# A four-layer graph network on one core: the first two groups of graphs interleaved, the last group finished by pairs

## The chip, the cores and the metric

The kernel runs on one core of a Trainium2 chip. The metric is the device time in microseconds (us), given as the median of the runs. The engines are named as in the profile: PE is TensorE's matmul, PEld its weight load, DVE is VectorE, ACT is ScalarE, POOL is GpSimd and SP is SyncE, which here issues nearly all DMAs. All data is fp32.

## The reference

`x` holds 128 graphs of 128 nodes with 512 features, `adj` their 128x128 adjacency matrices. Four layers follow one another, each as `x = layernorm(x + layer(x, adj))`, cut here to what is computed:

```python
# layer 0
Ah = A + I;  dh = rsqrt(sum(Ah, -1));  An = dh[:, :, None] * Ah * dh[:, None, :]
out = relu(einsum('bnm,bmf,fc->bnc', An, X, kernel) + bias)
# layer 1
q, k = split(x @ W_qk.T);  v = x @ W_v.T;  scores = q @ k.T / 8
out = softmax(sum(scores * A, -1), axis=nodes) * v
# layer 2
agg = (A @ x) / max(sum(A, -1), 1e-6)
out = relu(concat([x, agg]) @ W.T)
# layer 3
out = An @ (X @ W + b)
```

## The kernel before, in words

**Groups.** The 128 graphs are worked on in 32 groups of `G` = 4; the features of a group's four graphs lie in one SBUF tile `x` of 128 nodes by 4 x 512. A group goes through all four layers on chip, and is then stored.

**A layer.** `aggregate` (L441) multiplies x by the transposed adjacency matrix, so that the result comes out with the features on the partitions, as the next product needs it, and ScalarE copies it from PSUM (`agg<-p_agg`). Where a layer needs x itself in that form (layers 1 and 2), x has to be transposed: `turn_x` (L450) stores it to a scratch tensor in DRAM (`xT1s`, `xT2s`), loads it back in another order (`xT1y`, `xT2y`), and VectorE transposes blocks of 32x32. The adjacency matrices are transposed by TensorE for groups 0 and 1 (`prep_transpose`, L412, PSUM tile `p_a`) and by the same way over DRAM for the others (`prep_turn`, L423). `prep_rows` (L389) makes the scaled matrices: VectorE sums the degrees (`deg`, `dh`), GpSimd raises them to the power -1/2 (`d`), and VectorE multiplies (`ana`).

**A projection.** `project` (L482) is one step of a seven-product scheme (Strassen-Winograd): the two halves of the rows (graphs 0, 2 against 1, 3: the index `r`; `q` counts the pairs of graphs 0, 1 and 2, 3) and of the features make blocks, and seven products named B11, T1, B21, B22, T2, T3, T4 take the place of eight. Their left operands are sums made by `left_sums` (L464; GpSimd as a rule, tiles `xT1s`, `agg2s` and so on), their right ones sums of weight blocks made once by `weight_sums` (L359). Each product adds into a PSUM region `p_o` or `p_v`; VectorE combines the regions (`u_o`, `s_o`), adds to x, and takes the statistics of the layer norm (`norm_stats`, L568: VectorE `bno`, GpSimd `rstdo` and `mro`, ScalarE `nmro` and the scaling of x). For layer 3 ScalarE takes the statistics itself (`norm_last`, L550: `row`, `square`). The last product, T4, is put off: `project` leaves it in a list of tails, and the next projection runs it after its own first product (`finish_tails`). In PE's rows, `w_sb` stands for w0 and w3, so `p_o<-w_sb,agg` belongs to layer 0 or 3 by its time.

**The order of the work.** Every instruction is first recorded, then `Plan.schedule` (L192) puts them in order. TensorE's order is the program's. The other engines, the DMA issues on SP among them, take at each step the instruction that is ready and due first; a due time is counted back from TensorE's order with the costs of `estimate` (L279). A DMA counts 470 ns on SP and 1600 ns + size / 60 until it has landed, whatever else is under way. All planned instructions show line L258 in the profile.

The main loop (L764) runs over t and mixes group t with group u = t - 1: layer 0 of t, layer 2 of u (with the first half of t's qk), the aggregation of t + 1, layer 1 of t, the aggregation and projection of layer 3 of u, then x of t transposed over DRAM and aggregated for layer 2. So each group's norms and transposes have another group's products beside them. The ends have no such neighbour: before the loop group 0 is prepared and aggregated alone, at t = 0 only layers 0 and 1 of group 0 run, with group 1's preparation, and at t = 32 only layers 2 and 3 of group 31.

The loads: `load` (L334) brings `adj` and `x` of a group on SP's queue, `weight` (L344) a weight as four blocks of 256 KB or, turned, as 16 of 64 KB. w0 and b0 are issued by ScalarE, all else by SP.

Of the kernel before, what the change touches and what calls it, by code (L numbers as in the profile page):

```python
# [24 lines left out]
DEG_EPS = 1e-6  # L25

# [92 lines left out]
class Op:  # L119
    def __init__(self, engine):  # L120
        self.engine, self.dur, self.lat, self.calls, self.preds, self.succs = engine, 0, 0, [], set(), []
        self.last, self.start, self.end = float("inf"), None, None


class Plan:
# [5 lines left out]
    HOP = 200  # L131

# [22 lines left out]
    def record(self, engine, method, args, kw):  # L155
        op = self.group if self.group is not None and engine == "tensor" else Op(engine)
        op.calls.append((method, args, kw))
        dur, op.lat = self.est(engine, method, args, kw)
# [33 lines left out]
    def schedule(self):  # L192
# [24 lines left out]
        free = dict.fromkeys(self.ENGINES, 0)  # L217
# [5 lines left out]
        while len(done) < len(self.ops):  # L223
# [18 lines left out]
            free[e] = op.end  # L242
            if e == "tensor":
                pe.pop(0)
# [34 lines left out]
def estimate(engine, method, args, kw):  # L279
# [3 lines left out]
    if engine == "tensor":  # L283
        return (max(109, 0.85 * n) if method == "transpose" else 2 * max(100, 0.833 * n + 2.5)), 100
    if method == "dma_start":
        size = max(int(np.prod(v.shape)) if isinstance(v, bass.AP) else v.idx.size * 32 * len(v.quads) for v in args)
        return 470, 1600 + size / 60
    if engine == "scalar":
        return (380 if method == "activation" else 160) + 0.83 * n, 0
    if engine == "gpsimd":  # L290
        if ALU.pow in args:
            return 400 + 150 * n, 0
        return 250 + 2.2 * n, 0
# [3 lines left out]
    return 160 + (1.3 if len(both) > 1 else 1.04) * n, 0  # L297
# [4 lines left out]
def kernel(  # L302
# [15 lines left out]
    NT = B // G  # L318

# [14 lines left out]
    def load(t):  # L334
# [3 lines left out]
        nc.sync.dma_start(xi, x[t * G:(t + 1) * G].rearrange("g n f -> n g f"))  # L338
# [32 lines left out]
    make_identity(tc.nc, ident.real())  # L371
    nhalf = const.tile([P, G], FP, tag="nhalf", name="nhalf")
    nc.vector.memset(nhalf, -0.5)
    w0_sb = weight(w0, "w0_sb", nc.scalar)
    b0_sb = broadcast_row(b0, "b0_sb", nc.scalar)
# [88 lines left out]
    def left_sums(name, t, eng=nc.gpsimd):  # L464

        a = st[name, t].rearrange("p (q r) (h c) n -> p q r h c n", r=2, h=2)
        a11, a12, a21, a22 = a[:, :, 0, 0], a[:, :, 0, 1], a[:, :, 1, 0], a[:, :, 1, 1]
        s1, s2, s3, s4 = (tp.tile([P, 2, 2, P], FP, tag=f"s{i}", name=f"{name}s{i}_{t}", bufs=3) for i in (1, 2, 3, 4))
        eng.tensor_tensor(s1, a21, a22, ALU.add)
        eng.tensor_tensor(s2, s1, a11, ALU.subtract)  # L470
        eng.tensor_tensor(s3, a11, a21, ALU.subtract)
        eng.tensor_tensor(s4, a12, s2, ALU.subtract)
        st[name, t] = {B11: a11, B21: a12, B22: s4, T4: a22, T1: s1, T2: s2, T3: s3}
# [8 lines left out]
    def project(name, t, parts, first, c11, fin, hooks=None, after=lambda: None, early=True,  # L482
                when=lambda f: f()):
# [3 lines left out]
        hooks = hooks or {}  # L487

        def region():
            return ps_b.tile([P, 2, H], FP, tag="pb", name=f"p_{name}_{t}")  # L490

        def product(p, k, fresh):
            with nc.unit():
                for q in range(2):
                    for i, (left_, w) in enumerate(parts):
                        for c in range(2):
                            nc.tensor.matmul(p[:, q, :], left_[k][:, q, c, :], w[:, k, c, :],
                                             start=(fresh and q == 0 and i == 0 and c == 0),
# [4 lines left out]
        def block(tag):  # L503
            return tp.tile([P, 2, H], FP, tag=tag, name=f"{tag}_{name}_{t}", bufs=1 if tag in ("u5", "sb") else 2)
# [21 lines left out]
        when(lambda: (fin(0, 1, u2), norm_stats(name, t, 0)))  # L526
# [4 lines left out]
        def tail():  # L531
# [3 lines left out]
            norm_stats(name, t, 1)  # L535
# [4 lines left out]
    def half(z, r, h):  # L540

        return z.rearrange("p (q r) f -> p q r f", r=2)[:, :, r, h * H:(h + 1) * H]
# [7 lines left out]
    def norm_last(name, t, r):  # L550

        z = st["x", t]
        sm, nm, sq, rstd, nmr = (sp.tile([P, 2], FP, tag=f"last{i}", name=f"last{i}_{t}_{r}", bufs=2) for i in range(5))
        for q in range(2):
            row = tp.tile([P, F], FP, tag="row", name=f"row_{t}_{r}_{q}", bufs=1)
            nc.scalar.activation(row, z[:, 2 * q + r, :], AF.Copy, accum_out=sm[:, q:q + 1])
        nc.scalar.mul(nm, sm, -1.0 / F)
        for q in range(2):
            row = tp.tile([P, F], FP, tag="row", name=f"square_{t}_{r}_{q}", bufs=1)
            nc.scalar.activation(row, z[:, 2 * q + r, :], AF.Square, bias=nm[:, q:q + 1], accum_out=sq[:, q:q + 1])  # L560
        nc.gpsimd.tensor_scalar(rstd, sq, 1.0 / F, LN_EPS, ALU.mult, ALU.add)
        nc.gpsimd.tensor_tensor(rstd, rstd, nhalf[:, 0:2], ALU.pow)
        nc.gpsimd.tensor_tensor(nmr, nm, rstd, ALU.mult)
        for q in range(2):
            zg = z[:, 2 * q + r, :]
            nc.scalar.activation(zg, zg, AF.Identity, bias=nmr[:, q:q + 1], scale=rstd[:, q:q + 1])

    def norm_stats(name, t, r):  # L568
        if name == "o3":
            return norm_last(name, t, r)  # L570
        z = st["x", t]
        mv = sp.tile([P, 2, 2], FP, tag="mv", name=f"mv{name}_{t}_{r}")
        for q in range(2):
# [6 lines left out]
        nc.gpsimd.tensor_scalar(rstd, mv[:, :, 1], LN_EPS, None, ALU.add)  # L580
        nc.gpsimd.tensor_tensor(rstd, rstd, nhalf[:, 0:2], ALU.pow)
        nc.gpsimd.tensor_tensor(mr, mv[:, :, 0], rstd, ALU.mult)
        nc.scalar.mul(nmr, mr, -1.0)
        for q in range(2):
            zg = z[:, 2 * q + r, :]
            nc.scalar.activation(zg, zg, AF.Identity, bias=nmr[:, q:q + 1], scale=rstd[:, q:q + 1])


    def l0_agg(t, eng=nc.gpsimd):
# [3 lines left out]
        left_sums("agg0", t, eng)  # L593

    def relu_add(t):
        def fin(r, h, blk):
            z = half(st["x", t], r, h)
# [3 lines left out]
    def bias(h):  # L601
        return b0_sb[:, None, h * H:(h + 1) * H].to_broadcast([P, 2, H])

    def l0_out(t, hooks=None):
# [236 lines left out]
```

## Time and profile before

| What | Value |
|---|---|
| median of 3 runs | 2537.95 us (2536.98 to 2547.46) |
| profiled execution, own time | 2536.82 us |
| its span, first to last instruction | 2535.0 us |
| mean granted TensorE clock | 0.991 |
| DMA, mean over the span | 98 GB/s, 249.62 MB |
| PE busy in the first 60 us | 32.1 us |
| PE busy in the last 75 us (2460 to 2535) | 51.6 us |

The profile is one execution. A span row gives the busy time of each engine; a row of stretches gives the same for a part of the span, with the clock that TensorE was granted as a share of full speed. A wait row says which engine stood idle before which work, and what released it. A row of the timeline has the start, the length, the engine, the operation, out<-in with its shapes, the count, and in brackets the idle time just before. TensorE's rows count two instructions for each fp32 matmul of the program, and one for each transpose.

The first PE instruction starts at 12.42 us, the first product of layer 0 at 19.06. From 90.23 us PE works without a gap up to the steady part. At the end, the aggregation for layer 2 of the last group starts at 2460.58, the last matmul ends at 2521.47, ScalarE's last scaling at 2529.33, and the store of the last group's 1 MB lands at the span's end.

### The profile page before, as it was taken

To read this page: it belongs to the slowest core of one execution; us is meant where nothing else is said; L and a number is where in the kernel's file an instruction comes from. 1 tells how busy PE (TensorE), PEld (TensorE's weight loads), DVE (VectorE), ACT (ScalarE), POOL (GpSimd) and SP (SyncE) were. 2 spreads that over 40 slices of the span, in tenths; PEclk is the share of its full clock that TensorE was granted. 3 is DMA by queue.
4 is the path that set the end of the run, shared out by engine and by line. 5 is a ranking of instruction groups with operands and counts; after the bars stand their busy time and mean duration, and the time that the engine had idled before them with its cause. 6 is when DMAs were issued, how large, how long until landed. Compare 5 with 4: busy or idle time off the path is not lost.

```text
span 2535.0 us, 36875 instructions
## 1 busy us (share of the span) xinstructions
PE 2464.3 (97%) x13392; PEld 2201.8 (87%) x13392; DVE 1777.4 (70%) x3141; ACT 962.0 (38%) x1955; POOL 1354.6 (53%) x1522
## 2 busy tenths in 40 slices
PE   5899999999999999999999999999999999999996
PEld 4788888888888888888888888888988888888885
DVE  5677767776767776777777777767677767677663
ACT  1243334343334433343433343433443433344333
POOL 6455456464555564555554564655564645555542
PEclk8999999999999999999999999999999999999998
DMA  7233334324344324343333344233343243433120
GB/s 220 75 81 95 101 100 121 109 63 112 88 112 111 102 72 117 83 121 108 87 89 109 92 121 108 72 104 99 102 121 107 65 113 84 116 109 95 39 84 33
DMA packets 408532, 249.62 MB, mean 98 GB/s; under 512 B 141344, under 2 KB 375328, under 8 KB 408352
## 3 DMA queue, kind: packets, MB, share of 16 engines
q1 hardware_dynamic: 407120, 245.96, 36.0%
q8 instruction: 106, 1.74, 0.3%
q10 hardware_dynamic: 1232, 1.31, 0.2%
q14 instruction: 74, 0.61, 0.1%
HBM read 130.81 MB, written 116.39 MB: 98 GB/s over the span
## 4 chain that ended last, share of the span: by engine, by line
PE 75%; DVE 9%; DMA 5%; POOL 4%; issue 3%; SPq 2%; ACT 1%; ACTq 0%; DVEq 0%; POOLq 0%
PE p_o L258 45%; PE p_v L258 13%; PE p_agg L258 12%; DVE x L258 4%; PE p_qk L258 3%; SPq L258 2%; POOL xT2s L258 2%; ACT x L258 1%; DMA xT1y<-xT1s 1%; DMA adj<-in_adj_dram 1%; DVE u_o L258 1%; DMA xT1s<-x 1%; DVE s_v L258 1%; DVE ana L258 1%; DVE bnv L258 1%
## 5 line engine op out<-in xcount | busy, mean ns | idle before, releaser
L258 ACT COPY agg<-p_agg 128x512 f32<-128x512 f32 x384 | 224.9, 586 | 722.1 <-PE p_agg L258 722.1
L258 PE MATMUL p_o<-w_sb,agg 128*128 128x256 f32 x1536 | 354.8, 380 | 4.2 <-DVE u_o L258 2.2
L258 PEld LDWEIGHTS p_o<-w_sb,agg 128*128 128x128 f32 x1536 | 287.4, 191 | 42.6 <-ACT s_o L258 3.2
L258 POOL TENSOR_TENSOR xT1s<-xT 128x512 f32<-128x512 f32 x64 | 83.1, 1298 | 394.5 <-DVE xT L258 306.7
L258 POOL TENSOR_TENSOR agg3s<-agg 128x512 f32<-128x512 f32 x64 | 86.5, 1351 | 338.9 <-ACT agg L258 338.9
L258 PE MATMUL p_o<-w2x_sb,xT2s 128*128 128x256 f32 x1024 | 262.8, 379 | 0.0
L258 PE MATMUL p_o<-w2a_sb,agg2s 128*128 128x256 f32 x1024 | 262.8, 379 | 0.0
L258 PE MATMUL p_agg<-anT,x 128*128 128x128 f32 x2048 | 249.4, 281 | 10.0 <-ACT x L258 4.5
L258 PEld LDWEIGHTS p_agg<-anT,x 128*128 128x128 f32 x2048 | 240.2, 195 | 11.6 <-DVE anT L258 5.1
L258 PE MATMUL p_o<-w_sb,agg3s 128*128 128x256 f32 x1024 | 233.4, 381 | 5.6 <-DVE u_o L258 5.5
L258 PE MATMUL p_v<-wv_sb,xT1s 128*128 128x256 f32 x1024 | 233.3, 381 | 0.0
L258 PE MATMUL p_o<-w_sb,agg0s 128*128 128x256 f32 x1024 | 226.6, 379 | 2.9 <-DVE agg0s L258 1.9
L258 PEld LDWEIGHTS p_o<-w_sb,agg3s 128*128 128x128 f32 x1024 | 192.1, 190 | 41.7 <-POOL rstdv L258 16.8
L258 PEld LDWEIGHTS p_o<-w_sb,agg0s 128*128 128x128 f32 x1024 | 194.3, 190 | 30.1 <-POOL sb_o L258 2.2
L258 PEld LDWEIGHTS p_o<-w2x_sb,xT2s 128*128 128x128 f32 x1024 | 194.6, 190 | 26.5
L258 PEld LDWEIGHTS p_o<-w2a_sb,agg2s 128*128 128x128 f32 x1024 | 194.6, 190 | 26.4
L258 PEld LDWEIGHTS p_v<-wv_sb,xT1s 128*128 128x128 f32 x1024 | 189.6, 190 | 25.9
L258 POOL TENSOR_TENSOR agg2s<-agg 128x512 f32<-128x512 f32 x64 | 81.2, 1268 | 233.3 <-ACT agg L258 233.3
L258 PE MATMUL p_o<-w2x_sb,xT 128*128 128x256 f32 x768 | 198.3, 381 | 3.8 <-DVE xT L258 3.1
L258 DVE STREAM_TRANSPOSE xT<-xT1y 128x512 f32<-128x512 f32 x128 | 83.5, 690 | 168.4 <-DMA xT1y<-xT1s 168.4
L258 PE MATMUL p_o<-w2a_sb,agg 128*128 128x256 f32 x768 | 197.8, 380 | 0.0
L258 ACT ACTIVATE x<-x,nmro,rstdo 128x512 f32<-128x512 f32 x256 | 194.6, 807 | 4.8 <-ACT nmro L258 0.5
(116 smaller groups left out, 4705.8 us busy)
## 6 DMA issues: line engine op xcount, KB each, us to landing
x<-in_x_dram SPq DMA_DIRECT2D x32, 1024.0 KB, 6.2
xT1s<-x SPq DMA_DIRECT2D x128, 256.0 KB, 2.7
xT1y<-xT1s SPq DMA_DIRECT2D x256, 128.0 KB, 3.0
xT2s<-x SPq DMA_DIRECT2D x128, 256.0 KB, 2.6
xT2y<-xT2s SPq DMA_DIRECT2D x256, 128.0 KB, 3.3
out_dram<-x SPq DMA_DIRECT2D x32, 1024.0 KB, 5.5
sa<-ana SPq DMA_DIRECT2D x120, 128.0 KB, 3.4
ya<-sa SPq DMA_DIRECT2D x120, 128.0 KB, 3.7
```

Source lines behind the costliest of these rows:

```text
L258: getattr(getattr(self.nc, op.engine), method)(*[v.real() if isinstance(v, Ref) else v for v in args], **{k: v.real() if isinstance(v, Ref ...
```

## The change

- **First groups** (`begin`). Group 0 is prepared and its layer 0 starts; group 1's transposes and its aggregation lie between group 0's products of layer 0 (after B21 and B22). Then comes group 1's layer 0, ahead of group 0's layer 1. x of group 0 is transposed on TensorE for layers 1 and 2 (`turn_on_tensor`: a ScalarE copy that reorders the columns, four TensorE transposes into PSUM, a ScalarE copy out of it, for each graph), and `l2_both` mixes these transposes with the aggregation. qk of group 1 comes before that. The loop then starts at t = 1 without layer 0 and qk of group 1; its order from t = 2 on is the same.
- **Last group.** x of group 31 is transposed on TensorE (`l2_both`, with the sums of xT2 on VectorE). Layer 2 and layer 3 are run by pairs of graphs: 0, 1 first and then 2, 3, each with its own seven products of half the size. Each graph is stored as soon as it is scaled. The very last norm takes its statistics on VectorE.
- **Loads.** w0 and b0 are issued by SP too, x of group 0 comes in two halves, and the planner counts the DMAs on SP as sharing one bus of 95 elements per ns.
- **Clock.** 30 transposes of the identity matrix are put ahead of the first work of TensorE.
- Layer 0's sums for group 0 are made pair by pair.

```diff
+WARM = 30
...
+    LAND, BUS = 1600, 95
...
+            if e == "sync":
+                bus = max(bus, op.end + self.LAND) + op.size / self.BUS
+                op.lat = max(op.lat, bus - op.end)
...
-        return 470, 1600 + size / 60
...
         if ALU.pow in args:
...
-        nc.sync.dma_start(xi, x[t * G:(t + 1) * G].rearrange("g n f -> n g f"))
+        for g in range(0, G, 2 if t == 0 else G):
+            k = slice(g, g + (2 if t == 0 else G))
+            nc.sync.dma_start(xi[:, k], x[t * G:(t + 1) * G][k].rearrange("g n f -> n g f"))
...
+    p = ps_t.tile([P, C, P], FP, tag="pt", name="p_warm")
+    for _ in range(WARM):
+        nc.tensor.transpose(p[:, 0], ident, ident)
...
-    w0_sb = weight(w0, "w0_sb", nc.scalar)
-    b0_sb = broadcast_row(b0, "b0_sb", nc.scalar)
+    w0_sb = weight(w0, "w0_sb", nc.sync)
+    b0_sb = broadcast_row(b0, "b0_sb", nc.sync)
...
+    def turn_on_tensor(name, t, r, pairs=(0, 1)):
+
+        y = tp.tile([P, 2, C, P], FP, tag="y", name=f"{name}y_{t}_{r}", bufs=3)
+        for q in pairs:
+            g = 2 * q + r
+            z = y[:, q]
+            nc.scalar.copy(z.rearrange("p c (b j) -> p c b j", b=Q),
+                           st["x", t][:, g, :].rearrange("p (b c j) -> p c b j", b=Q, c=C))
+            p = ps_t.tile([P, C, P], FP, tag="pt", name=f"p_{name}_{t}_{g}")
+            with nc.unit():
+                for c in range(C):
+                    nc.tensor.transpose(p[:, c, :], z[:, c], ident)
+            nc.scalar.copy(st[name, t][:, g], p)
+
+    def left_sums(name, t, eng=nc.gpsimd, pairs=(slice(0, 2),)):
...
+        s = [tp.tile([P, 2, 2, P], FP, tag=f"s{i}", name=f"{name}s{i}_{t}", bufs=3) for i in (1, 2, 3, 4)]
+        for q in pairs:
+            a11, a12, a21, a22 = a[:, q, 0, 0], a[:, q, 0, 1], a[:, q, 1, 0], a[:, q, 1, 1]
+            s1, s2, s3, s4 = (v[:, q] for v in s)
+            eng.tensor_tensor(s1, a21, a22, ALU.add)
+            eng.tensor_tensor(s2, s1, a11, ALU.subtract)
+            eng.tensor_tensor(s3, a11, a21, ALU.subtract)
+            eng.tensor_tensor(s4, a12, s2, ALU.subtract)
+        st[name, t] = {B11: a[:, :, 0, 0], B21: a[:, :, 0, 1], B22: s[3], T4: a[:, :, 1, 1], T1: s[0], T2: s[1], T3: s[2]}
...
-                for q in range(2):
+                for q in pairs:
                     for i, (left_, w) in enumerate(parts):
                         for c in range(2):
-                            nc.tensor.matmul(p[:, q, :], left_[k][:, q, c, :], w[:, k, c, :],
-                                             start=(fresh and q == 0 and i == 0 and c == 0),
+                            nc.tensor.matmul(p[:, q - pairs[0], :], left_[k][:, q, c, :], w[:, k, c, :],
+                                             start=(fresh and q == pairs[0] and i == 0 and c == 0),
                                              stop=(i == len(parts) - 1 and c == 1), skip_group_check=True)
...
-        when(lambda: (fin(0, 1, u2), norm_stats(name, t, 0)))
+        when(lambda: (fin(0, 1, u2), norm_stats(name, t, 0, pairs)))
...
-            norm_stats(name, t, 1)
+            norm_stats(name, t, 1, pairs)
             after()
...
+        for q in pairs:
             zg = z[:, 2 * q + r, :]
             nc.scalar.activation(zg, zg, AF.Identity, bias=nmr[:, q:q + 1], scale=rstd[:, q:q + 1])
-
-    def norm_stats(name, t, r):
-        if name == "o3":
-            return norm_last(name, t, r)
+            if t == last:
+                nc.sync.dma_start(out[t * G + 2 * q + r], zg)
+
+    def norm_stats(name, t, r, pairs):
+        if name == "o3" and (t, r, pairs[-1]) != (last, 1, 1):
...
+        for q in pairs:
             zg = z[:, 2 * q + r, :]
             nc.scalar.activation(zg, zg, AF.Identity, bias=nmr[:, q:q + 1], scale=rstd[:, q:q + 1])
-
-
-    def l0_agg(t, eng=nc.gpsimd):
+            if name == "o3":
+                nc.sync.dma_start(out[t * G + 2 * q + r], zg)
...
         left("xT1", t)
         for r in range(2):
-            turn_x("xT1", t, r)
+            turn("xT1", t, r)
...
+
+        left("xT2", t)
+        left("agg2", t)
+        for r in range(2):
+            turn_on_tensor("xT2", t, r)
+            for g in (r, 2 + r):
+                aggregate("agg2", t, g, st["arT", t])
+        left_sums("xT2", t, nc.vector)
+        left_sums("agg2", t)
...
+    def l3_agg_pair(t, q, eng):
+        left(f"agg3{q}", t)
+        for g in (2 * q, 2 * q + 1):
+            aggregate(f"agg3{q}", t, g, st["anT", t])
+        left_sums(f"agg3{q}", t, eng, ONE_BY_ONE[q:q + 1])
...
+        project("o3", t, [(st[left, t], w3_sb)], copy_first, lambda p, b: fin(0, 0, p), fin,
+                after=lambda: store(t), pairs=pairs)
 
     def store(t):
+        if t == last:
+            return
         nc.sync.dma_start(out[t * G:(t + 1) * G].rearrange("g n f -> n g f"), st["x", t])
...
-    prep_rows(0)
-    load(1)
-    prep_transpose(0)
-    weight_sums(w0_sb, nc.gpsimd)
-    l0_agg(0, nc.vector)
...
-    for t in range(NT + 1):
...
+    def begin():
+
+        prep_rows(0)
+        load(1)
+        prep_transpose(0)
+        weight_sums(w0_sb, nc.gpsimd)
+        l0_agg(0, nc.vector, ONE_BY_ONE)
+        prep_rows(1)
+        l0_out(0, {B21: [lambda: prep_transpose(1)], B22: [lambda: l0_agg(1)]})
+        finish_tails()
+        weight_sums(wv_sb, nc.vector)
+        l0_out(1)
+        l1_turn(0, turn_on_tensor)
+        finish_tails()
+        for r in range(2):
+            l1_qk(0, r)
+        for w in (w2x_sb, w2a_sb, w3_sb):
+            weight_sums(w, nc.gpsimd)
+        l1_turn(1)
+        l1_out(0, {B11: [lambda: l1_scores(0)], B21: [lambda: l1_softmax(0)], T3: []})
+        finish_tails()
+        for r in range(2):
+            l1_qk(1, r)
+        l2_both(0)
+
+    begin()
+    for t in range(1, NT):
...
-        if a:
+        if t > 1:
             l0_out(t)
-        if more:
-            if b:
-                load(t + 1)
+        if t < last:
+            load(t + 1)
             prep_rows(t + 1)
-            if b:
-                prep_turn(t + 1)
-        if a:
+            prep_turn(t + 1)
+        if t > 1:
             tails.append(lambda: l1_turn(t))
-        if a and b:
-            l2_out(u, {T3: [lambda: l1_qk(t, 0)]})
-        elif b:
-            l2_out(u)
-        else:
-            weight_sums(wv_sb, nc.vector)
-            for w in (w2x_sb, w2a_sb, w3_sb):
-                weight_sums(w, nc.gpsimd)
-            finish_tails()
-            prep_transpose(t + 1)
-        if more:
+        l2_out(u, {T3: [lambda: l1_qk(t, 0)]} if t > 1 else {})
+        if t < last:
             l0_agg(t + 1)
         finish_tails()
-        if a:
-            if not b:
-                l1_qk(t, 0)
+        if t > 1:
             l1_qk(t, 1)
-        if a:
-            l1_out(t, {B11: [lambda: l1_scores(t)], B21: [lambda: l1_softmax(t)],
-                       T3: [lambda: l3_agg(u)] if b else []})
-        elif b:
-            l3_agg(u)
-        if b:
-            l3_bias(u)
-            l3_out(u)
-        else:
-            finish_tails()
-        if a:
+        l1_out(t, {B11: [lambda: l1_scores(t)], B21: [lambda: l1_softmax(t)], T3: [lambda: l3_agg(u)]})
+        l3_bias(u)
+        l3_out(u)
+        if t < last:
             l2_turn(t)
             l2_agg(t)
+
+    l2_both(last)
+    for q in range(2):
+        l2_out(last, pairs=(q,))
+    for q in range(2):
+        l3_agg_pair(last, q, nc.gpsimd)
+        l3_bias(last, (2 * q, 2 * q + 1))
+        l3_out(last, f"agg3{q}", (q,))
     finish_tails()
```

## The prediction

> **What bounds the kernel now.** I read the busy shares first, then the busy time by stretches, then the waits of TensorE, then its timeline at both ends.
>
> ```profile
> PE 2464.3 (97%) x13392; PEld 2201.8 (87%) x13392; DVE 1777.4 (70%) x3141; ACT 962.0 (38%) x1955; POOL 1354.6 (53%) x1522
> ```
>
> TensorE (PE) is busy in 97% of the span, so only 70.7 us of idle time, and whatever a lowered clock cost, can be won. The stretches tell where it lies (columns: stretch, length, busy us of PE, PEld, DVE, ACT, POOL with counts, granted clock, DMA share, GB/s):
>
> ```profile
> 100.00:2400.00 2300.00, 2288.15 (x12522) 2048.07 (x12522) 1655.01 (x2926) 896.59 (x1825) 1246.90 (x1401) 1.00 0.37 98
> 20.00:50.00 30.00, 19.50 (x93) 16.09 (x91) 26.54 (x40) 6.06 (x11) 24.02 (x21) 0.89 0.78 238
> 46.00:47.00 1.00, 1.00 (x7) 0.50 0.07 22
> 47.00:48.00 1.00, 0.80 (x6) 0.85 0.00 1
> ```
>
> Between 100 and 2400 us PE idles 11.9 us; the other 59 us lie in the first 100 us and the last 75, the places that the change rewrites. The last two rows (PE only) show the other loss: after an idle gap the clock is 0.50 until some us of work have passed. The waits of PE name the gaps (us in total, times, longest):
>
> ```profile
> PE p_a L258 <- DVE ana L258: 12.4, 1, 12.4
> PE p_agg L258 <- ACT x L258: 10.5, 3, 4.5
> PE p_o L258 <- DVE u_o L258: 9.4, 33, 1.4
> PE p_w L258 <- DVE rs L258: 6.3, 7, 1.6
> PE p_qk L258 <- issue: 4.8, 1, 4.8
> PE p_agg L258 <- DVE anT L258: 4.5, 1, 4.5
> PE p_o L258 <- DVE xT L258: 3.1, 1, 3.1
> ```
>
> **Rates at full clock**, from PE's timeline: 4 projection matmuls 1.73 us (a layer of one part 12.1, layer 2 24.2), one aggregation of four graphs 3.57, qk 3.56, four transposes 0.45. At the start 90.23 us hold work worth: transposes 1.8, three aggregations 10.7, layer 0 of group 0 12.1, qk 3.56, scores and softmax 1.05, v 12.1, first product of group 1 1.7: 43.0. So 47.2 us are lost there.
>
> **First stretch, step by step.** The likeliest course, in us from the span's start.
>
> *Loads and first transposes.* p_a waits for ana, which waits for d on POOL; d stood behind a weight sum of w0 (POOL 8.34 to 9.6) that found its data because w0 came on ACT's queue beside x. Now w0 follows adj and x on SP's queue. adj has landed at 5.1 as before; deg and dh end at 6.0; d (1.03) finds POOL free, 7.1; the multiplication 0.7 (1.75 took it beside a POOL sum): p_a at 7.9, not 12.42. The loads move at about 380 GB/s from 4 to 8 us, so adj, x and w0 (2.3 MB) are in by 9, before the first product. On the cost side, w0's and b0's five loads and x's second half go onto SP, six issues at 0.45 (2.7 us), ahead of wqk and wv, which are wanted after 40.
>
> The Trainium skill (DMA: Bandwidth & Descriptors, Issuing engines are not separate DMA queues) says that queues share the same 16 engines, so another queue only saves the issuer's time. By that rule the move to one queue gains nothing in rate, and here only the order can pay: the 4.5 us come from d's place on POOL. Were d behind a sum after all, 1.3 of them would go.
>
> *Warm-up transposes.* 30 of them, at some 0.22 us while cold (p_a's 8 took 1.97 us cold, 1.04 later), run from about 1.5 to 8 us, when PE has nothing else. The Trainium skill (TensorE: Matmul & The Clock Gate, Part 4: PE-mode transpose) says that transposes do not count as PE work for the clock; then they gain nothing and might hold p_a up by 0.3. The trace speaks against it: the first 32 aggregation instructions took 4.74 us to the next, against 3.57 warm, hence 2.3 us cold, and full clock came at 16.7. Counted from the transposes at 12.42 that is 4.2 us, in line with 4.7 from 42.66 in the rows above; counted without them, 2.3 is shorter than any other warm-up I find (3.5 to 6.1). I take them as counting, near that row: 1.2 us won in the aggregation (up to 0.9 more in p_a is left out); ends -0.3 and 2.1.
>
> So p_a 7.9, anT and aggregation as before 1.9 later, 9.8, and the first product at 13.5 (19.06 before).
>
> *Layer 0 of group 0.* 18.2 us before for 12.1 of work (waits for agg0s, s_o, u_o). Now group 1's transposes (0.9) and aggregation (3.57) lie inside it: 16.6, plus 3 of waits that stay, as DVE is the busiest engine here (26.54 of 30): 33.1. What followed before is gone as a place to wait: 4.49 for anT, 4.84 at qk, 1.03 for agg.
>
> *Group 1's layer 0 as cover.* Its six products (10.4, with 1.4 of waits) run to 44.9 while x of group 0 is normalized; before, its second half was ready 11.2 us after the last product (37.1 to 48.3), and 33.1 + 11.2 is 44.3. Then 16 transposes (1.8, new, with 0.5 for ScalarE's copies), the last product 1.7, qk 3.6: 52.5. The two DMA trips of the old turn are off the path. New on ScalarE: 8 copies of 0.59, hidden, as it was busy 6.06 of 30.
>
> *Layer 1 of group 0 and layer 2's inputs.* v and scores 13.1 plus 0.9 as before: 66.5. Then qk of group 1 (3.6) fills to 70.1; its x goes by DMA; in the middle its second half is transposed 16.6 after the last product (180.7 to 197.4), here at 48.8 + 16.6 = 65.4, just ahead of its qk at 68.3. Before, PE waited 4.41 and 1.62 for x, with a lowered clock between: 8.4 lost. The first half of x is there 4.5 after the last product (71), the second after 9 (75.5), each with a copy of 0.6 ahead of its transposes; two times 0.9 + 1.8 of PE work, the last copy 0.6, some 1.5 for the clock: layer 2 starts at 81.
>
> Before, the same work would stand done at 90.23 + 10.4 (rest of layer 0) + 3.56 (qk) = 104.2, and PE had no gap there. **Start: 23 us**; DVE is tight, so 22.
>
> **Middle.** PE's order is unchanged from group 2 on; the planner's new DMA estimate may shift other engines' orders. Of its 11.9 us idle, the waits for rs and u_o hang on no DMA. I take 0; ends -3 and +6.
>
> **End.** From 2460.58 (aggregation of layer 2) to 2521.47 (last product) 60.9 us pass for 45.2 of work.
>
> ```profile
> 2467.38 2.08 PE L258 MATMUL p_o<-w2x_sb,xT 128*128 128x256 f32 x4 [3.06 <-DVE xT L258]
> 2469.25 1.78 PE L258 MATMUL p_o<-w2a_sb,agg 128*128 128x256 f32 x4
> 2502.55 3.78 PE L258 MATMUL p_agg<-anT,x 128*128 128x128 f32 x16 [4.51 <-ACT x L258]
> 2506.12 2.98 PE L258 MATMUL p_o<-w_sb,agg 128*128 128x256 f32 x8
> ```
>
> In brackets the gaps; 1.78 where 1.03 is usual and 3.78 for 16 where 1.8 is usual is the lowered clock. The first gap with its clock costs 3.06 + 1.75, the second 4.51 + 2.0 + 1.06: 12.4 together. TensorE's turn takes away the first (x's second half ended at 2459.7, two DMA trips and DVE at 2467.3), for 1.8 of transposes and 0.6 for the last copy. The second was the norm's chain after the last product; by pairs, pair 0 is normalized while pair 1 multiplies (8.7 us of PE against a chain of 6.2), and pair 1's chain (4.6 for one graph) lies behind five products of layer 3's pair 0, 0.86 each: about 0.5 is left. Halved DVE instructions (0.42 for 256 elements, 0.69 for 512) add 20%, in a stretch where DVE idles 2.7 us per product; the sums of xT2 move from POOL onto it (4 of 0.69) into that idle time. 12.4 - 2.4 - 0.5 = 9.5; **8** taken, for waits as short as the 0.78 ones, of which pairs have more.
>
> After the last product, 13.5 us before: sum and add 1.4, ScalarE's statistics 3.5, then scaling to 2529.33, and a 1 MB store landing 5.5 later. Now for one graph: 0.42 + 0.42, statistics on DVE 0.85, POOL 1.1, ScalarE 1.0, hops 0.6, issue 0.5, landing 2.7 as the other 256 KB transfers: 7.6. The three earlier stores of 256 KB are issued by SP while PE multiplies, with nothing queued behind them but the last. **6 us**.
>
> **Sum.** 22 + 0 + 8 + 6 = 36 on the profiled execution's own 2536.82 (span 2535.0): 2500.8. The median of the runs is 1.1 above it: 2502.
>
> **Rivals.**
> *VectorE becomes the bound of the start.* Between 20 and 50 us it did 26.5 us of work, 23.3 without group 2's rows. Group 1's layer 0 adds 11.5: 34.8 to do between 9.7 and 46. For it: 88% busy, and instructions of 1.75 instead of 0.69 beside POOL's sums. Against it: 4.4 of it (sums of wv) can come later. With a sixth of its time lost between dependent steps, group 0's qk is 6 late: 2508.
> *The pairs do not cover the norms.* The chain per pair is as long as before but for halved bn and scaling, and POOL (rstd 0.65 + 1.07 beside its sums) may be late. Then the end wins what is left of the first gap (2.4) and 5 of the tail, 7 less: 2509.
> *Slower: the new DMA estimate reorders SP's queue.* Place: the turn of x for layer 1 in each of 30 groups. Its first half is transposed at 190.6 for qk at 197.93 (slack 7.3), its second at 197.4 for 206.8. Were the 1 MB store (5.5 to landing) and the 1 MB load (6.2) both issued ahead, it would land 11.7 late, 4.4 of PE per group, 132 in all: 2634. It decides from 8.5 us late (1.2 per group eats the 36). Against it: only ready times change, never due times, and both behind one another move 2 MB in some 5.5 us.
> *It does nothing.* PE's order itself is changed, so only if the gaps are refilled by waits of the same length: 2538.
> *Everything is hidden*: no norm gap at 70 to 80, no DVE waits: 45 won, 2493.
>
> **Chances.** Forecast (2494 to 2507) 0.58; VectorE 0.17; pairs 0.11; everything hidden 0.08; nothing 0.04; slower 0.02. The range runs from 2490 (all hidden, -3 in the middle) to 2516 (both first rivals together with a little of the middle). 0.5%, about what a measurement of this kernel can tell, is 12.7 us: faster 0.94, same 0.04, slower 0.02.
>
> **What would show it.** Right: p_a near 8 with instructions of 0.11; no wait of PE for anT or at qk; layer 2 of group 0 at 78 to 84; PE gaps for x under 2 us in the last 75; about 8 us from the last matmul to the end. Wrong: a clock of 0.50 in the start's windows after 20 us, DVE above 90% from 14 to 45 with PE waiting for it, or a PE idle time between 100 and 2400 well above 12 us.

## The result, and the profile after

| kernel | runs | median (range), us | to before [95%] |
|---|---|---|---|
| before | 4 | 2537.47 (2536.68 to 2547.46) | |
| after | 4 | 2507.39 (2505.78 to 2508.08) | 0.9872 [0.9847, 0.9897] |

(The median of before moved from 2537.95 to 2537.47 with a fourth run.) The change saves 30.1 us, 1.2%; the forecast was 36 (2502). The profiled execution took 2507.6 us, with a span of 2505.8 against 2535.0 before: 29.2 less. First the busy shares of the kernel after, whose planned instructions show line L263 (L258 before):

```profile
PE 2466.6 (98%) x13470; PEld 2204.4 (88%) x13470; DVE 1785.2 (71%) x3161; ACT 973.2 (39%) x1981; POOL 1350.2 (54%) x1530
```

TensorE is busy 2.3 us longer than before (78 instructions more: the turns and the warm-up) in a span 29.2 us shorter: 31.5 us of idle time went, and 39.2 of the 70.7 are left. The stretches of the kernel after, with the columns as before; the last two rows are TensorE's stretch of the last group, of the kernel after and of before:

```profile
100.00:2400.00 2300.00, 2291.12 (x12522) 2050.61 (x12521) 1649.55 (x2923) 895.50 (x1823) 1249.20 (x1404) 1.00 0.37 97
20.00:50.00 30.00, 24.58 (x120) 20.89 (x121) 24.08 (x35) 4.68 (x9) 21.55 (x20) 0.89 0.69 210
22.00:24.80 2.80, 1.93 (x8) 1.59 (x9) 2.77 (x5) 0.00 (x0) 1.26 (x1) 0.50 0.62 164
2448.78:2497.70 48.92, 47.97 (x257) 41.93 (x255) 29.51 (x56) 27.79 (x62) 20.39 (x36) 1.00 0.07 27
```

```profile
2460.58:2521.60 61.02, 51.06 (x241) 43.97 (x239) 24.44 (x39) 21.69 (x46) 20.56 (x24) 0.92 0.14 40
```

The end is solved: 0.95 us idle at a clock of 1.00, where before had 10 idle at 0.92. The start is not: between 20 and 50 us TensorE still idles 5.4 of 30, and the clock falls to 0.50 once more, which the prediction had named as a sign of being wrong. The waits of TensorE, after:

```profile
...
PE p_a L263 <- DVE ana L263: 6.1, 2, 5.5
PE p_xT L263 <- ACT xT2y L263: 6.0, 2, 5.5
...
PE p_qk L263 <- DVE xT L263: 1.5, 2, 1.1
```

The waits of 12.4 (ana), 10.5 (x), 4.8 (qk), 4.5 (anT) and 3.1 (xT) are gone. Two new ones of 5.5 stand in their place, both in the first 90 us. TensorE's timeline of the start shows where, and what follows each:

```profile
7.11 1.04 PE L263 MATMUL p_a<-ident,ana 128*128 128x128 f32 x8
8.50 3.84 PE L263 MATMUL p_agg<-anT,x 128*128 128x128 f32 x32 [0.35 <-DVE anT L263]
...
22.28 1.09 PE L263 MATMUL p_a<-ident,ana 128*128 128x128 f32 x4 [5.55 <-DVE ana L263]
...
24.84 6.35 PE L263 MATMUL p_o<-w_sb,agg0s 128*128 128x256 f32 x24
...
89.62 1.97 PE L263 MATMUL p_xT<-ident,xT2y 128*128 128x128 f32 x8 [5.54 <-ACT xT2y L263]
91.38 3.62 PE L263 MATMUL p_agg<-arT,x 128*128 128x128 f32 x16
94.80 1.20 PE L263 MATMUL p_o<-w2x_sb,xT 128*128 128x256 f32 x4
```

After both gaps the clock must be earned again: 24 matmuls take 6.35 us where 5.35 is usual (the 24 of v from 66.79), and 16 of an aggregation 3.62 instead of 2.05. Layer 2 of group 0 starts at 94.80, not at 81.

The first gap waits for ana of group 1. VectorE's, POOL's and SP's timelines of the kernel after (VectorE's first row is the same product for group 0):

```profile
6.08 0.69 DVE L263 TENSOR_TENSOR ana<-ana,d 128x512 f32<-128x512 f32 x1 [0.63 <-POOL d L263]
...
18.00 0.69 DVE L263 TENSOR_REDUCE deg<-adj 128x4 f32<-128x512 f32 x1 [1.57 <-DMA adj<-in_adj_dram]
...
20.39 1.74 DVE L263 TENSOR_TENSOR ana<-ana,d 128x512 f32<-128x512 f32 x1 [0.62 <-POOL d L263]
22.06 1.75 DVE L263 TENSOR_TENSOR ana<-adj,rdeg 128x512 f32<-128x512 f32 x1
```

```profile
20.33 1.26 POOL L263 TENSOR_TENSOR sb_o<-s_o,b_sb 128x512 f32<-128x512 f32 x1
21.66 1.60 POOL L263 TENSOR_TENSOR s_o<-s_o,b_sb 128x512 f32<-128x512 f32 x1
```

```profile
12.02 0.38 SPq L263 DMA_DIRECT2D adj<-in_adj_dram  x1
```

The adjacency of group 1 is issued only at 12.02, since its buffer is group 0's (one of a kind), and is there at 18. VectorE's two products of 128x512 then take 1.74 and 1.75 us where 0.69 is usual, while POOL adds the bias to sb_o and s_o.

The second gap waits for the second half of x for layer 2, which waits for VectorE's last additions of layer 1. VectorE's and POOL's rows there:

```profile
79.30 1.50 DVE L263 SCALAR_TENSOR_TENSOR x<-s_v,ws,x 128x256 f32<-128x256 f32 x1
80.73 1.50 DVE L263 SCALAR_TENSOR_TENSOR x<-u_v,ws,x 128x256 f32<-128x256 f32 x1
```

```profile
79.16 1.36 POOL L263 TENSOR_TENSOR xT1s<-xT 128x512 f32<-128x512 f32 x1 [0.55 <-DVE xT L263]
80.60 1.34 POOL L263 TENSOR_TENSOR xT1s<-xT1s,xT 128x512 f32<-128x512 f32 x1
```

While POOL's sums run, from 79.16 to 83.35, an addition takes 1.50 us instead of 0.44 to 0.48. There are three such, the third from 82.15: 3 us on the chain that ends the gap.

By stage, from the two traces: the start (to layer 2 of group 0; before's equal point is 104.2) gave 104.2 - 94.8 = 9.4, forecast 22. The middle gave 2.4, forecast 0. The end gave 74.4 - 57.0 = 17.4, forecast 14: till the last matmul 60.9 became 48.9, and the 13.5 after it became 8.1. Together 29.2.

### The profile page after: what moved, and what is told of

Read it like the earlier page. It is cut to its first block, busy times and chain, and to the rows that moved or that the text cites. A ratio compares the mean times of both kernels' runs of the same rounds, so it can differ in the third digit from the quotient of the medians.

```text
span 2505.8 us, 37042 instructions
## 1 busy us (share of the span) xinstructions
PE 2466.6 (98%) x13470; PEld 2204.4 (88%) x13470; DVE 1785.2 (71%) x3161; ACT 973.2 (39%) x1981; POOL 1350.2 (54%) x1530
## 3 DMA queue, kind: packets, MB, share of 16 engines
q8 instruction: 107, 1.75, 0.3%
## 4 chain that ended last, share of the span: by engine, by line
PE 75%; DVE 10%; DMA 5%; POOL 4%; SPq 2%; issue 2%; ACT 2%; DVEq 0%; ACTq 0%; POOLq 0%
PE p_o L263 44%; PE p_v L263 14%; PE p_agg L263 12%; DVE x L263 4%; PE p_qk L263 3%; SPq L263 2%; POOL xT2s L263 2%; ACT x L263 1%; DMA xT1s<-x 1%; DVE u_o L263 1%; DMA xT1y<-xT1s 1%; DMA adj<-in_adj_dram 1%; DVE bnv L263 1%; DVE s_v L263 1%; PE p_sc L263 1%
## 5 line engine op out<-in xcount | busy, mean ns | idle before, releaser
L263 ACT COPY agg<-p_agg 128x512 f32<-128x512 f32 x384 | 225.2, 586 | 730.0 <-PE p_agg L263 730.0
L263 PE MATMUL p_o<-w_sb,agg 128*128 128x256 f32 x1536 | 353.7, 379 | 2.7 <-ACT s_o L263 1.4
L263 PEld LDWEIGHTS p_o<-w_sb,agg 128*128 128x128 f32 x1536 | 286.4, 190 | 40.5 <-ACT s_o L263 2.2
L263 POOL TENSOR_TENSOR xT1s<-xT 128x512 f32<-128x512 f32 x64 | 84.1, 1315 | 381.1 <-DVE xT L263 369.0
L263 PE MATMUL p_o<-w2x_sb,xT2s 128*128 128x256 f32 x1024 | 262.8, 379 | 0.0
L263 PE MATMUL p_o<-w2a_sb,agg2s 128*128 128x256 f32 x1024 | 262.8, 379 | 0.0
L263 POOL TENSOR_TENSOR agg3s<-agg 128x512 f32<-128x512 f32 x62 | 84.1, 1357 | 330.0 <-ACT agg L263 330.0
L263 PE MATMUL p_agg<-anT,x 128*128 128x128 f32 x2048 | 243.9, 277 | 0.3 <-DVE anT L263 0.3
L263 PEld LDWEIGHTS p_agg<-anT,x 128*128 128x128 f32 x2048 | 235.4, 192 | 1.3 <-DVE anT L263 0.6
L263 PE MATMUL p_v<-wv_sb,xT1s 128*128 128x256 f32 x1024 | 233.3, 381 | 0.0
L263 PE MATMUL p_o<-w_sb,agg3s 128*128 128x256 f32 x992 | 226.6, 381 | 5.8 <-DVE u_o L263 5.7
L263 PE MATMUL p_o<-w_sb,agg0s 128*128 128x256 f32 x1024 | 227.7, 380 | 1.0 <-DVE u_o L263 1.0
L263 PEld LDWEIGHTS p_o<-w_sb,agg3s 128*128 128x128 f32 x992 | 185.9, 190 | 41.4 <-POOL rstdv L263 17.4
L263 PEld LDWEIGHTS p_o<-w_sb,agg0s 128*128 128x128 f32 x1024 | 195.2, 191 | 28.0 <-DVE u_o L263 1.4
L263 PEld LDWEIGHTS p_o<-w2x_sb,xT2s 128*128 128x128 f32 x1024 | 194.6, 190 | 26.5
L263 PEld LDWEIGHTS p_o<-w2a_sb,agg2s 128*128 128x128 f32 x1024 | 194.6, 190 | 26.4
L263 PEld LDWEIGHTS p_v<-wv_sb,xT1s 128*128 128x128 f32 x1024 | 189.6, 190 | 26.2
L263 POOL TENSOR_TENSOR agg2s<-agg 128x512 f32<-128x512 f32 x64 | 81.9, 1280 | 236.1 <-ACT agg L263 236.1
L263 DVE STREAM_TRANSPOSE xT<-xT1y 128x512 f32<-128x512 f32 x124 | 80.9, 690 | 168.1 <-DMA xT1y<-xT1s 168.1
L263 PE MATMUL p_o<-w2x_sb,xT 128*128 128x256 f32 x768 | 197.4, 379 | 0.7 <-ACT s_o L263 0.7
L263 ACT ACTIVATE x<-x,nmro,rstdo 128x512 f32<-128x512 f32 x257 | 195.9, 807 | 4.4 <-DVE dm L263 0.2
L263 PE MATMUL p_o<-w2a_sb,agg 128*128 128x256 f32 x768 | 197.1, 379 | 0.0
```

The lines of the kernel that those rows point to most:

```text
L263: getattr(getattr(self.nc, op.engine), method)(*[v.real() if isinstance(v, Ref) else v for v in args], **{k: v.real() if isinstance(v, Ref ...
```

## The experiments

The forecast fell short in the start alone. **Theory A**: the two gaps have the causes just read, the late load into a shared buffer and POOL's sums beside VectorE, and each can be taken away. **Theory B**: VectorE, by its work or by contention, bounds the start; a gap that is closed opens elsewhere. Each run below is set against the runs of before on the same chip: its median in the first four 2536.02, in e5 to e8 2536.24, in e9 to e11 2538.25, in e12 2536.12. The kernel after itself ran beside e9 and e11 alone (as e10); for the others, differences to its 2507.39 go across chips or times of measurement. In brackets stands the ratio to before with its 95% interval.

**e1: a buffer of its own for group 1's adjacency.**

```diff
-        a = ap.tile([P, G, P], FP, tag="adj", name=f"adj_{t}", bufs=1)
+        if t == 1:
+            a = tp.tile([P, 2, G, P], FP, tag="y", name="adj_1", bufs=3)[:, 0]
+        else:
+            a = ap.tile([P, G, P], FP, tag="adj", name=f"adj_{t}", bufs=1)
```

> The changed kernel with one difference: the adjacency matrices of group 1 get a buffer of their own (they share one with group 0's, so that their load waits for group 0's to be read). Theory A (the start lost its gain to this late load: it was issued at 12.02 and landed at 17.95, and TensorE waited 5.55 + 0.59 us for ana and then worked at a lowered clock): the load lands by about 8, the two waits go, group 0's layer 0 ends 6 to 7 us earlier and the whole is 5 to 7 us faster than the changed kernel (about 2501). Theory B (VectorE and GpSimd bound the start): the waits for ana are replaced by waits for u_o and the gain is below 2 us.

2507.46 us (2505.24 to 2508.22), 0.9884 [0.9869, 0.9899]: no gain, and layer 2 of group 0 starts at 92.57. The wait for ana is gone, but TensorE's timeline shows another at 24.62, with the lowered clock behind it (8 matmuls in 3.78 us, 1.89 being usual):

```profile
24.62 3.78 PE L263 MATMUL p_o<-w_sb,agg0s 128*128 128x256 f32 x8 [2.61 <-DVE u_o L263]
```

```profile
13.45 1.75 DVE L263 TENSOR_TENSOR ana<-ana,d 128x512 f32<-128x512 f32 x1 [0.91 <-POOL d L263]
15.11 2.90 DVE L263 TENSOR_TENSOR agg0s<-agg 128x256 f32<-128x256 f32 x2
```

VectorE's rows (second fence) say why: the sums for group 0 now stand behind the products for ana, and the first four take 1.45 us each beside POOL's sums of w0 and its bias additions, where later ones take 0.38. Theory A alone falls here: B is right that the gap moves, by contention.

**e2: the sums of xT1 of group 1 on VectorE instead of POOL.** (`l1_turn` and its `left_sums("xT1", t, eng)` get the engine as an argument.)

```diff
-        l1_turn(1)
+        l1_turn(1, eng=nc.vector)
```

> The changed kernel with one difference: the sums of xT1 for group 1 are made on VectorE, not on GpSimd. Theory A (the second gap, 5.54 us for the second half of x of group 0 ahead of layer 2, comes from VectorE's last additions of layer 1 taking 1.5 us each, not 0.48, beside GpSimd's sums): the additions take 0.48 each, x is there 3 to 4 us earlier, and the whole is 3 to 5 us faster than the changed kernel. Theory B (the chain of the norm itself is that long, whatever GpSimd does): less than 1 us, since VectorE gets 2.8 us more work.

2503.31 (2503.0 to 2503.9), 0.9869 [0.9855, 0.9884]: 4 us less than after, and than e1 beside it (2507.46, the fastest 2505.24), with more work on VectorE. Its rows, then TensorE's:

```profile
79.13 0.48 DVE L263 SCALAR_TENSOR_TENSOR x<-s_v,ws,x 128x256 f32<-128x256 f32 x1
```

```profile
86.79 1.18 PE L263 MATMUL p_xT<-ident,xT2y 128*128 128x128 f32 x8 [2.89 <-ACT xT2y L263]
87.80 2.04 PE L263 MATMUL p_agg<-arT,x 128*128 128x128 f32 x16
```

The additions are back at 0.48, the gap is 2.89 instead of 5.54, and the aggregation after it runs at full clock. The second cause is shown.

**e3: no warm-up transposes.**

```diff
-    for _ in range(WARM):
-        nc.tensor.transpose(p[:, 0], ident, ident)
```

> The changed kernel without the 30 transposes of the identity. If transposes count for the clock: p_a's 8 take about 2.0 us and the first aggregation 4.7 (1.04 and 3.7 with them), so the first product starts at about 14.3, not 12.2. The 2 us should then vanish in the wait for ana at 22 us, which does not hang on TensorE: the whole is the same within 0.5 us. If the time is a sum of TensorE's parts it is 2 us slower.

2509.76 (2509.34 to 2514.43), 0.9894 [0.9878, 0.9911]. Without them p_a's 8 take 1.97 us and the first aggregation 5.72 (1.04 and 3.84 with them):

```profile
6.92 1.97 PE L263 MATMUL p_a<-ident,ana 128*128 128x128 f32 x8 [6.92 <-DVE ana L263]
8.82 5.72 PE L263 MATMUL p_agg<-anT,x 128*128 128x128 f32 x32
```

The first product starts at 14.38 instead of 12.17: the transposes do raise the clock and bring 2.2 us there. The wait for ana that follows takes them back (3.24 long instead of 5.55). Layer 2 of group 0 starts at 93.81, between the 92.59 (e10) and the 94.80 of the kernel after: in the start nothing is left of them. The total is another matter: the expected "same within 0.5 us" did not come, for e3's fastest run, 2509.34, is slower than the slowest of after, 2508.08, and of e1 beside it, 2508.22. In its profiled run, the slowest, the extra time lies in the middle (2361.8 us against 2354.0), for which no cause is shown.

**e4: the new start with the old end** (layers 2 and 3 of the last group in the order of before, one store of 1 MB).

```diff
-    l2_both(last)
-    for q in range(2):
-        l2_out(last, pairs=(q,))
...
+    l2_turn(last)
+    l2_agg(last)
+    l2_out(last)
...
```

> The changed kernel with the end of the kernel before: group 31 transposed over DRAM, layers 2 and 3 for all four graphs at once, statistics of the last norm on ScalarE, one store of 1 MB. By the windows of the two traces the end is worth 17.4 us of the 29.2, the start 9.4 and the middle 2.4: about 2525. If the forecast's split (start 22, end 14) were right after all and the windows misread, it would be 2521 or less.

2521.15 (2518.93 to 2523.25), 0.9939 [0.9925, 0.9954]: 14.9 us in all, where the two traces give start and middle 11.8. But not all of it is start and middle: in e4's trace the last group takes 71.2 us, not before's 74.4, in before's order. There x came back from DRAM sooner, and the gap that cost before 3.06 us and 1.75 of clock was shorter:

```profile
2454.69 1.13 PE L263 MATMUL p_o<-w2x_sb,xT 128*128 128x256 f32 x4 [1.71 <-DVE xT L263]
2455.66 1.03 PE L263 MATMUL p_o<-w2a_sb,agg 128*128 128x256 f32 x4
```

Without these 3.2 us start and middle are worth about 11.7, as in the two traces; whether the planner's DMA estimate or that one execution made the turn quicker was not tried. Layer 2 of group 0 started at 91.3 here, in the same order of work as after's 94.8.

**e5: the old start, loads and planner with the new end.**

```diff
-    begin()
...
+    prep_rows(0)
+    load(1)
+    prep_transpose(0)
+    weight_sums(w0_sb, nc.gpsimd)
+    l0_agg(0, nc.vector)
...
```

> The kernel before with the new end alone: group 31 transposed on TensorE, layers 2 and 3 by pairs, stores by graph, last statistics on VectorE; its loads, its start and its planner are those of before. By the windows of the two traces the end is worth 17.4 us: 2520 where the kernel before takes 2537.5, a ratio of 0.993. The forecast's 14 would be 2523.5.

2519.63 (2517.55 to 2521.44), 0.9935 [0.992, 0.9949]: 16.6 us for the end, near the 17.4 of the traces. With e4's 14.9 that makes 31.5 against 30.1, and 28.3 without the 3.2 of the last group: to within 2 us the two parts add up.

**e6: the planner's old DMA estimate.**

```diff
-            if e == "sync":
-                bus = max(bus, op.end + self.LAND) + op.size / self.BUS
-                op.lat = max(op.lat, bus - op.end)
```

> The changed kernel with the planner's old estimate of a DMA (no shared bus). The forecast put the middle at 0, -3 to +6: if that holds, the middle (from layer 2 of group 0 to the turn of group 31, 2354.0 us with the bus) is the same within 2 us, and the whole the same within 3. If the bus estimate earns what the middle gained against the kernel before (2.4), it is slower by that.

2506.66 (2505.85 to 2510.73), 0.9887 [0.9872, 0.9902]: nothing that can be measured in the total. VectorE's and POOL's order in the start is another one, and layer 2 of group 0 starts at 92.45. Its profiled run, the slowest, has a middle of 2359.5 us, outside the 2 us expected, but that length differs by some us between executions of one kernel too (2354.0 in after, 2356.7 in e10).

**e7: e1 and e2 together, and the sums of w0 on VectorE too.**

```diff
-        weight_sums(w0_sb, nc.gpsimd)
+        weight_sums(w0_sb, nc.vector)
```

> The changed kernel with three differences: group 1's adjacency matrices in a buffer of their own, and the sums of w0 and of group 1's xT1 on VectorE in place of GpSimd. Theory A (the first stretch is bound by VectorE while GpSimd's sums run beside it: its two-input instructions took 1.75 us there, 0.69 alone): the sums of agg0 take 0.4 per half, not 1.45, the wait for u_o of 2.6 us that replaced the wait for ana goes, and layer 2 of group 0 starts at 84 to 87 (94.8 in the changed kernel, 89.7 with group 1's sums on VectorE alone): about 2500. Theory B (VectorE's own work is the bound, whoever runs beside it): 2.8 us more work on VectorE make it no faster than the 2503 of the run with group 1's sums alone.

2502.69 (2501.37 to 2503.19), 0.9867 [0.9853, 0.9882], no better than e2 alone. Layer 0 of group 0 now ran without a long wait, and a new one stood in group 1's. POOL's rows, then TensorE's:

```profile
30.55 5.97 POOL L263 TENSOR_TENSOR w2a_sb<-w2a_sb 128x512 f32<-128x512 f32 x4 [13.07 <-DMA w2a_sb<-in_L_gnn_W_dram]
...
38.15 1.25 POOL L263 TENSOR_TENSOR agg0s<-agg 128x512 f32<-128x512 f32 x1
```

```profile
39.46 5.41 PE L263 MATMUL p_o<-w_sb,agg0s 128*128 128x256 f32 x16 [4.50 <-POOL agg0s L263]
```

POOL works in order. It stood 13 us before a sum of w2 whose data had not come, and group 1's agg0s, wanted by TensorE, stood behind that (e9, below, starts it at 26.97).

**e8: the last group without the pairs** (turn on TensorE, stores by graph and VectorE's last statistics kept).

```diff
-    for q in range(2):
-        l2_out(last, pairs=(q,))
-    for q in range(2):
-        l3_agg_pair(last, q, nc.gpsimd)
-        l3_bias(last, (2 * q, 2 * q + 1))
-        l3_out(last, f"agg3{q}", (q,))
+    l2_out(last)
+    finish_tails()
+    l3_agg(last)
+    l3_bias(last)
+    l3_out(last)
```

> The changed kernel with the last group's layers 2 and 3 for all four graphs at once; the turn on TensorE, the stores by graph and the statistics of the last norm on VectorE stay. If pairs cover the norm between layer 2 and layer 3, the gap of about 4.5 us for x and its lowered clock (3 us more) come back, and the last norm scales two graphs, not one: 8 to 9 us slower than the changed kernel, about 2516. If the gap was short for another reason (the turn on TensorE alone), 2 us slower at most.

2516.44 (2515.62 to 2517.37), 0.9924 [0.9907, 0.994]: 9 us more than after (e6, beside it, took 2506.66), and the end is 65.9 us long in its trace instead of 57.0. Before's gap is back:

```profile
2486.99 3.46 PE L263 MATMUL p_agg<-anT,x 128*128 128x128 f32 x16 [4.51 <-ACT x L263]
```

So the pairs bring 9 of the end's 17.4, 1.2 of them behind the last matmul (9.3 became 8.1), where one graph is left to normalize instead of two; the turn, the stores and the statistics bring the other 8.5.

**e9: e7, with POOL's sums of w2 and w3 put behind group 1's bias additions.** `op.preds` holds what the planner must place first.

```diff
+        anchor = [op for op in nc.ops if op.engine == "gpsimd" and op.calls[0][0] == "tensor_tensor" and op.calls[0][2] == {} and b0_sb.tile in [v.tile for v in op.calls[0][1][:3] if isinstance(v, Ref)]][-1]
+        first_sum = len(nc.ops)
         for w in (w2x_sb, w2a_sb, w3_sb):
             weight_sums(w, nc.gpsimd)
+        for op in nc.ops[first_sum:]:
+            op.preds.add(anchor)
```

> The changed kernel with four differences: a buffer of its own for group 1's adjacency matrices, the sums of w0 and of group 1's xT1 on VectorE, and the planner told to put GpSimd's sums of w2 and w3 behind group 1's bias additions. Theory A (what is left of the start's loss is order: in the run with the first three, GpSimd waited for w2a's load until 30.5 with the sums of group 1's aggregation queued behind, and TensorE waited 4.50 us for them): that wait and the lowered clock after it go, layer 2 of group 0 starts at 81 to 83 as forecast, and the whole is 5 to 7 us faster than the run with three differences: about 2496. Theory B (GpSimd has too much work in the start whatever its order): the sums of w2 delay xT1's or the norms, and it is not faster than 2501.

2495.87 (2494.35 to 2496.7), 0.9831 [0.9817, 0.9846]: faster than both kernels, 42 us below before. Layer 2 of group 0 starts at 80.41:

```profile
80.41 1.03 PE L263 MATMUL p_o<-w2x_sb,xT 128*128 128x256 f32 x4
```

The stretch from 10 to 50 us, of e9 and then of the kernel after:

```profile
10.00:50.00 40.00, 37.87 (x226) 33.69 (x225) 36.22 (x60) 14.26 (x28) 26.80 (x24) 1.00 0.71 210
```

```profile
10.00:50.00 40.00, 30.64 (x157) 25.84 (x157) 30.94 (x44) 7.30 (x14) 27.84 (x24) 0.91 0.73 210
```

VectorE is 91% busy and TensorE 95%, where the slower kernel after has 77% for both: the amount of VectorE's work is not the bound. B holds only as contention and as order.

**e10: the kernel after once more, beside e9.**

> The changed kernel unchanged, for a comparison on the same chip: 2507 by all theories; the time at which layer 2 of group 0 starts shows how much the start differs from run to run.

2506.58 (2504.86 to 2508.03), 0.9872 [0.9856, 0.9889]. Layer 2 of group 0 started at 92.59; both gaps were the same (5.56 and 5.54).

**e11: e9 with the shared adjacency buffer again** (e9 without e1's edit).

> The same as the run with all differences, but group 1's adjacency matrices share the buffer of group 0's again. Theory A (the late load of the adjacency matrices costs its full wait once VectorE is not held up): TensorE waits about 5 us for ana again, its clock falls, and the whole is 6 to 8 us slower than with all differences. Theory B (another wait takes its place, as with the buffer alone in the changed kernel): at most 2 us slower.

2504.16 (2503.4 to 2505.31), 0.9865 [0.985, 0.988]: 8.3 us more than e9 beside it, from an edit that alone was worth nothing (e1). The gap is back:

```profile
21.74 1.09 PE L263 MATMUL p_a<-ident,ana 128*128 128x128 f32 x4 [5.31 <-DVE ana L263]
```

**e12: e9 without the warm-up transposes** (e3's edit).

> The run with all four differences (2495.9), without the 30 transposes of the identity. There no wait for ana stands behind the first aggregation, so that 2 us lost at the start should show: the first product at 14.3, not 12.1, and layer 2 of group 0 at 82.5, not 80.4; the whole about 2498. If the waits that are left (for u_o, for x before layer 2) take up the 2 us, it is 2496 again.

2498.22 (2494.81 to 2499.01), 0.9847 [0.9833, 0.986], against e9's [0.9817, 0.9846]. In the trace the first product is 1.85 us later (13.93 against 12.08), and so is everything down to the transposes for layer 2 (77.85 against 75.97). Then e9's next 16 matmuls ran at a lowered clock, those of e12 not; e9's two rows, then e12's:

```profile
75.97 1.34 PE L263 MATMUL p_xT<-ident,xT2y 128*128 128x128 f32 x8 [2.88 <-ACT xT2y L263]
77.10 3.47 PE L263 MATMUL p_agg<-arT,x 128*128 128x128 f32 x16
```

```profile
77.85 1.18 PE L263 MATMUL p_xT<-ident,xT2y 128*128 128x128 f32 x8 [2.88 <-ACT xT2y L263]
78.86 2.04 PE L263 MATMUL p_agg<-arT,x 128*128 128x128 f32 x16
```

The same gap of 2.88 us lowered the clock in one execution and not in the other. The medians differ by 2.4 us, each beside other runs of before, and the intervals overlap: whether the transposes show in the total stays open.

## Why the prediction was right, and where it was not

The sign, the places and most mechanisms held. The total, 2507.4, came 5 us above the forecast, just past the range that was given 0.58 (to 2507) and beside the 2508 of the VectorE rival. That it came so near is in part luck: by the traces the start fell 12.6 short, and the middle and the end gave 2.4 and 3.4 more than forecast. The term that failed is "Start: 22". Its steps, as durations in us from the trace of after:

| step | forecast | after | what made the difference |
|---|---|---|---|
| to the first product | 13.5 | 12.2 | warm-up worth 2.2, not 1.2 |
| layer 0 of group 0 | 19.6 | 26.9 | late adjacency, slow VectorE, clock |
| group 1's six products | 11.8 | 12.6 | s_o 0.7, u_o 1.0 |
| turn of x (16 transposes) | 2.3 | 3.6 | ScalarE's copies |
| last product, qk | 5.3 | 5.3 | |
| v of group 0 | 14.0 | 14.1 | |
| qk of group 1 | 3.6 | 5.8 | waits of 0.49 and 1.06 for xT |
| x in two halves | 10.9 | 14.3 | slow additions, clock |
| sum: layer 2 starts | 81 | 94.8 | |

*Loads and first transposes.* Right in the result: p_a stood at 7.11 (7.9) in warm instructions, eight in 1.04 us. The reason was not whole: d's place on POOL was to bring it all, with the adjacency landed "at 5.1 as before". VectorE could read it at 3.67, and at 3.49 to 3.85 in the eleven other kernels with the new loads, against 5.11 before and 4.81 in e5 with the old ones; that is 1.4 us which the working had put at nothing.

*Warm-up.* Right in kind; the 2.2 us in e3 are past the upper end given, 2.1. The Trainium skill (TensorE: Matmul & The Clock Gate, Part 4: PE-mode transpose) has it that transposes do not count as work for the clock; here the measurement decides, and e3 and e12 show that these fp32 transposes do count (the first aggregation took 5.72 and 5.46 us without them, 3.84 with them).

*Layer 0 of group 0.* The step that failed most. "3 of waits that stay" came from VectorE's load in the trace of before, where group 1's rows were prepared later and their buffer was no matter. The prediction moved the transposes of group 1 to 17 us and did not ask when their input could be loaded. It knew 1.75 for 0.69 beside a POOL sum, and charged it to the rival alone, not to the sum. With all four edits the step took 18.4 us (e9), inside the forecast.

*Layer 1 and layer 2's inputs.* The second gap was foreseen (first half of x at 71, second at 75.5), but the times came from rows of the middle, where no POOL sums run beside the last additions. e2 shows that this cost 2.65 us of the gap, and the clock after it.

*Middle.* Right: from layer 2 of group 0 to the last group it took 2356.4 us before and 2354.0 after, but 2356.7 when the kernel after ran again (e10), so the 2.4 us are no gain of the change. It is 2353.9 to 2361.8 in all fourteen traces, which share its order of work; what moves it was not tried.

*End.* Right in kind and 3.4 too low. By the working 9.5 was to be won before the last matmul, and 8 was taken for fear of short waits; 12.0 came. The last copy for the turn (0.6) and the pairs' 0.5 did not show, and the halved instructions left waits of 0.39 and 0.52 where before had 0.78, 0.68 and 0.78. The tail gave 5.4, forecast 6: 8.1 from the last matmul, forecast 7.6. By the medians of e5 the whole end is worth 16.6, 2.6 above the forecast.

*The rivals.* "VectorE becomes the bound of the start" was the nearest (2508), and its place was right. Of its two reasons the slowed instructions held (e2). The amount of work did not: from 14 to 45 us VectorE was busy 25.0 of 31 (81%, where 90% was named as a sign), and with more VectorE work e9 is 10.7 us faster than e10 beside it. "The pairs do not cover the norms" and the slower one fell; no wait for a turn in the middle was new.

That the start could give what was forecast is shown by e9: layer 2 at 80.4 for 81, and 2495.9 in total. But it took four edits at once. Single ones brought nothing (e1), 4 us (e2) or, as a set without the order on POOL, no more than e2 (e7), while one taken from the full set cost 8.3 (e11). That some 2 to 4 us of the start vary between executions of one order (94.80, 92.59 in e10, 91.33 in e4) is measured. Between the first two, 1.0 is the clock after the second gap (16 of the aggregation in 3.62 and 2.63) and the rest short waits from 47 to 55 us; what sets them was not tried.

## What to carry to other kernels

When a step is moved forward, follow its inputs back to their DMA and ask what holds that buffer then: here a single-buffered load of 256 KB cost 8 us once the other waits were gone (e9, e11). Where waits stand one behind another, an edit that brings nothing alone can still be needed: try it again with the others, and take it away from the full set. Work given to an idle engine is not free when it slows the busy one: price it by rows in which both run.

## What was not expected of the hardware

VectorE instructions with two inputs in SBUF take 2.5 to 4 times as long beside POOL's tensor_tensor sums: 0.69 became 1.75 (128x512), 0.48 became 1.50 (the additions of 128x256), 0.38 became 1.45 (sums of 128x256, e1). In the rows above it looks like waiting and not like a lower rate: the two additions from 79.30 end 0.28 and 0.29 us after the POOL sum beside them, the two products from 20.39 end 0.54 and 0.55 after theirs. Four POOL sums of 1.3 us, moved to VectorE at 0.7 each, made the kernel 4 us faster (e2).

The same gap of 2.9 us before x's second half stands in five runs. From its end to layer 2 passed 2.89 us in e2 and e12, and 4.29 to 4.44 in e7, e9 and e11, at a lowered clock (0.61 from 76.0 to 80.4 in e9). That makes such a gap worth between 2.9 and 4.4 us.
